# A cross-attention kernel: queries as seven products of halves, and the softmax's division applied to the product with the values

## The chip, the cores and the metric

The kernel runs on one core of a Trainium2 chip. The metric is the device time in microseconds (us) of one execution; lower is better. Times below are medians of several executions, or come from one execution that the hardware profiler recorded.

## The reference

There are 16 samples of 1024 query rows and 64 context rows, 512 features, 16 heads of 32. In short:

```python
xq  = (1 + scale_q(t)) * layernorm(x_q)  + shift_q(t)     # per sample: a scale and shift per feature
xkv = (1 + scale_kv(t)) * layernorm(x_kv) + shift_kv(t)
q   = xq @ Wq + bq                       # 1024 x 512 per sample
k,v = split(xkv @ Wkv + bkv)             # 64 x 512 each
attn = softmax(q k^T / sqrt(32))         # per head, over 64 keys
out  = x_q + (attn @ v) @ Wp + bp
```

Everything is float32.

## The kernel before

Work is cut into 32 blocks of 512 query rows, two for each sample. A block i passes through these stages, named by the functions that issue them:

- `load_x` brings x to SBUF; `q_stats`, `q_scale` and `hidden` normalise its rows (DVE statistics, small ACT and POOL steps, ACT normalising).
- `turn` transposes 32x32 squares on DVE into `ht`, and `move` puts them in their places with 16 DMAs between SBUF tiles, issued on SyncE's queue (SP). The result `xt` has features on partitions; its pool holds two buffers.
- `queries(i, o)` for o = 0 to 3 multiplies `xt` with weights that carry the sample's scale (`query_weights`, ACT, once for each sample): four matmuls on 512 columns for each o. ACT evicts each with its bias into `qt`.
- `scores(i, z)` for two halves z of the keys: 32x32-tiled matmuls into PSUM; DVE takes maxima per query and head, ACT copies the scores to SBUF. `maxima` spreads the maxima over the keys' partitions with one DVE transpose, `subtract` takes them off (POOL, two instructions of 128x2048), `weights` is the exponential (ACT, one for each z).
- `sums` adds up over keys (DVE, one for each z), `inverse` forms the reciprocals and spreads them (DVE transpose into `vb`), `divide` multiplies both halves of the weights by them (POOL, two instructions of 128x2048).
- `mix` multiplies with the values into PSUM (`po`).
- The projection with Wp is done as seven products of halves already (Strassen's scheme in Winograd's order): `mixed_halves` copies out of PSUM (ACT), `row_sums` and `last_row_sum` form sums of the mixed rows (DVE, one on POOL), `product(i, 1..7)` are the seven products, each 8 matmul instructions on 256 columns, in PSUM banks 2 and 3 seeded with the bias by `biased`, and `added(i, n)` adds each partial result to the residual `r` (DVE) and starts the output DMA.
- `context_features`, `keys`, `value_products` and `value_tiles` treat two samples' context once every four blocks.

A float32 matmul appears as two instructions in the profile. The whole kernel is one straight program whose order is written out by hand (`manual_schedule`): every engine and SP's queue execute their instructions in the order in which the Python code issues them, and wait on semaphores for the rest. The steady part is `for i in range(3, NB - 2)`, line 898. A "period" below is one turn of that loop: it does the scores of block i, the queries of block i+1, the mix and most of the projection of block i-1, the rest of the projection of i-2, the turning of i+2 and the load of i+3.

Instructions on one SP queue are all the loads, all the output stores and the 16 DMAs of each `move`.

Lines that the prediction uses: 487 query matmuls (`pq`), 504 their eviction (`qt`), 515 score matmuls (`ps`), 526 maxima, 533 score copies, 547 the spreads (`mb`, `vb`), 560 subtract, 566 exponential, 571 sums, 591 divide, 611 mix (`po`), 638 plain projection, 682 `residual_rest`, 702 and 703 `mixed_halves`, 710 to 714 `row_sums`, 719 `last_row_sum`, 740 the products (`pp`), 754 `added`, 756 the stores, 452 the DMAs of `move`, 132 and 139 the loads of x and of the residual, 169 small bias loads (`b_v_sb`), 347 and 375 the key and value products, 388 the values' eviction.

Of the kernel before, what the change touches and what calls it, by code (L numbers as in the profile page):

```python
# [15 lines left out]
P = 128  # L16
# [4 lines left out]
def cross_attention_block(  # L21
# [41 lines left out]

    nc = tc.nc
# [20 lines left out]
    big = ctx.enter_context(tc.tile_pool(name="big", bufs=4))  # L85
# [58 lines left out]
    def load_scale_shift(name, w):  # L144
        for j in range(2):
            t = big.tile([P, NC, H], F32, tag="big", name=f"wss_{name}_{j}")
            nc.sync.dma_start(t, w[:, j * H : (j + 1) * H].rearrange("(c p) o -> p c o", p=P))
            w_ss[name, j] = t
# [5 lines left out]
    at = 0  # L154
# [99 lines left out]
    def rstd_of(mv, n, tag, apart):  # L254
# [6 lines left out]
        rstd = small.tile([P, 2, n], F32, tag=f"rstd{tag}", name=f"rstd{tag}")  # L261
        work = small.tile([P, 4, n], F32, tag=f"work{tag}", name=f"work{tag}")
# [18 lines left out]
        return rstd  # L281

    q_mv, kv_mv, q_rstd, kv_rstd = {}, {}, {}, {}

    def q_stats(i, ts=range(NT)):
        if ts[0] == 0:
            q_mv[i] = small.tile([P, NT, 2], F32, tag="mvq", name=f"mvq_{i}")
        for t in ts:
            row_stats(q_mv[i][:, t, :], x_tiles[i][:, t, :])

    def q_scale(i):
        q_rstd[i] = rstd_of(q_mv.pop(i), NT, "q", i > 1)
# [5 lines left out]
    def kv_scale(b):  # L298
        kv_rstd[b] = rstd_of(kv_mv.pop(b), 1, "k", b > 0)
# [18 lines left out]
    def context_hidden(b):  # L318
        hk = kvpool.tile([P, H], F32, tag="hk", name=f"hk_{b}")
        normalise(hk, ctx_tiles.pop(b), kv_rstd.pop(b), 0)  # L320
        hk_tiles[b] = hk

    def context_features(b):
        hk = hk_tiles.pop(b)
        pt = bank(f"pkt_{b}")
        for c in range(NC):
            nc.tensor.transpose(pt[:, c * P : (c + 1) * P], hk[:, c * P : (c + 1) * P], ident)
        xk = kvpool.tile([P, NC, P], F32, tag="xk", name=f"xk_{b}")
# [11 lines left out]
        xk_tiles[b] = xk  # L340

    def keys(b):
        xk = xk_tiles[b]
        pk = bank(f"pk_{b}")
        for o in range(NC):
            for c in range(NC):
                nc.tensor.matmul(  # L347
                    pk[:, o * P : (o + 1) * P],
                    lhsT=w_kv_sb[:, c, o * P : (o + 1) * P],
                    rhs=xk[:, c, :],  # L350
                    start=(c == 0),
                    stop=(c == NC - 1),
                )
        kt = kvpool.tile([P, NC, P], F32, tag="kt", name=f"kt_{b}", bufs=2)
# [11 lines left out]
    def value_products(b):  # L366

        xk = xk_tiles.pop(b)
        pv = bank(f"pv_{b}").rearrange("p (j z f) -> p j z f", j=2, z=2)
# [107 lines left out]
    def queries(i, o, spare=False, later=False):  # L477

        xt, b = xt_tiles[i], i // BPB
        if o == 0:  # L480
            qt_tiles[i] = qpool.tile([P, NC, TB], F32, tag="qt", name=f"qt_{i}")
        if spare:
            pq = ps_s.tile([P, 2, TB], F32, tag="s", name=f"pq_{i}_{o}")[:, 0, :]
        else:
            pq = bank(f"pq_{i}_{o}")
        for c in range(NC):
            nc.tensor.matmul(  # L487
                pq.rearrange("p (g n) -> p g n", g=4),
                lhsT=wq_tiles[b][:, c, o * P : (o + 1) * P],
# [8 lines left out]
    def queried(i, o):  # L498
# [5 lines left out]
        nc.scalar.activation(dst, pq, AF.Identity, bias=bqs[:, o, b : b + 1])  # L504
# [3 lines left out]
    def scores(i, z):  # L508
# [15 lines left out]
        s_sb = big.tile([P, HPC, TB], F32, tag="big", name=f"s_{i}_{z}")  # L524
        for e in range(2):
# [6 lines left out]
            )  # L532
            nc.scalar.copy(s_sb[:, 2 * e : 2 * e + 2, :], pss[e])  # L533
        s_tiles[i, z] = s_sb
# [53 lines left out]
    def divide(i, eng=nc.gpsimd):  # L588
        vb = vb_tiles.pop(i)
        for z in range(2):  # L590
            eng.tensor_tensor(s_tiles[i, z], s_tiles[i, z], vb, ALU.mult)  # L591

# [64 lines left out]
    HO, HT, HC = H // 2, TB // 2, NC // 2  # L657
# [5 lines left out]
    def weight_sums():  # L663
        t1, t2, t3, t4 = (WT[:, j] for j in range(4))
        nc.gpsimd.tensor_tensor(t1, half_weights(0, 1), half_weights(0, 0), ALU.subtract)
        nc.gpsimd.tensor_tensor(t2, half_weights(1, 1), t1, ALU.subtract)
        nc.gpsimd.tensor_tensor(t3, half_weights(1, 1), half_weights(0, 1), ALU.subtract)
        nc.gpsimd.tensor_tensor(t4, half_weights(1, 0), t2, ALU.subtract)
        nc.gpsimd.tensor_tensor(b_diff, b_first, b_second, ALU.subtract)


# [4 lines left out]

    def twice(b):
        return b.unsqueeze(1).to_broadcast([P, 2, HO])

    def residual_rest(i):  # L680
        r = r_tiles[i][:, 2:, :HO]
        nc.gpsimd.tensor_tensor(r, r, twice(b_diff), ALU.add)

    acc = {}

    def biased(i):

        for k, n, b in ((2, 1, b_second), (3, 2, b_diff)):
            acc[k] = bank(f"pp_{i}_{n}", k)
            nc.scalar.copy(acc[k].rearrange("p (t h) -> p t h", t=2), twice(b))  # L690

# [6 lines left out]
    def mixed_halves(i):  # L698

        ot_tiles[i] = opool.tile([P, NC, TB], F32, tag="ot", name=f"ot_{i}")  # L700
        first, second = po_tiles[i]
        nc.scalar.copy(ot_tiles[i][:, HC:, :], second)
        nc.scalar.copy(half_rows(i, 0, 0), first[:, :, :HT])

    def row_sums(i):

        first = po_tiles.pop(i)[0]
        s1_tiles[i] = opool.tile([P, HC, HT], F32, tag="s1", name=f"s1_{i}")
        s2_tiles[i] = opool.tile([P, HC, HT], F32, tag="s2", name=f"s2_{i}")
        nc.vector.tensor_tensor(s1_tiles[i], first[:, :, HT:], half_rows(i, 1, 1), ALU.add)  # L710
        nc.vector.tensor_tensor(
            half_rows(i, 1, 0), half_rows(i, 0, 0), first[:, :, HT:], ALU.subtract
        )
        nc.vector.tensor_tensor(s2_tiles[i], s1_tiles[i], first[:, :, :HT], ALU.subtract)

    def last_row_sum(i):

        a12 = half_rows(i, 0, 1)
        nc.gpsimd.tensor_tensor(a12, a12, s2_tiles[i], ALU.subtract)

    def product(i, n, first=False):
# [4 lines left out]
            3: (lambda: half_rows(i, 0, 1), half_weights(1, 1)),  # L726
            4: (lambda: half_rows(i, 1, 1), WT[:, 3]),
            5: (lambda: s1_tiles.pop(i), WT[:, 0]),
            6: (lambda: s2_tiles[i], WT[:, 1]),
# [4 lines left out]
        new = n == 7 or first and n < 3  # L734
        if new:
            acc[k] = bank(f"pp_{i}_{n}", k)
        for t in range(2):
            for c in range(HC):
# [5 lines left out]
                    start=new and t == 0 and c == 0,  # L744
# [4 lines left out]
    def added(i, n):  # L749

        m, o = {1: (0, 0), 2: (0, 0), 6: (1, 0), 7: (1, 1), 5: (1, 1), 4: (1, 0), 3: (0, 1)}[n]
# [75 lines left out]
    queries(1, 3)  # L827
    sums(0, 1)
# [63 lines left out]
    residual(2, (0, 1))  # L892
    context_features(2)
    query_weights(2)
# [3 lines left out]
    for i in range(3, NB - 2):  # L898
        nxt3 = i + 3 < NB
        kvb = i // 4 * 2 + 2  # L900
        kv = i % 4 if kvb < B else None
        if nxt3:
            load_x(i + 3)
        if kv == 0:
            load_context(kvb)
        if i > 3:
            added(i - 2, 5)
        scores(i, 0)
        if i > 3:
            product(i - 2, 4)  # L910
            added(i - 2, 4)
            product(i - 2, 3)
            added(i - 2, 3)
        else:
            project(i - 2, 3)
            ring[:] = [0, 1]
        scores(i, 1)
        maxima(i)
        subtract(i)
        queries(i + 1, 0)  # L920
        load_residual(i)
        if i > 3:
            biased(i - 1)
        hidden(i + 2, (0, 1))
        mix(i - 1)
        mixed_halves(i - 1)
        hidden(i + 2, (2, 3))
        if kv == 1:
            context_hidden(kvb)
        if nxt3:  # L930
            q_stats(i + 3)
        if kv == 0:
            kv_stats(kvb)
        row_sums(i - 1)
        turn(i + 2, range(NT))
        move(i + 2)
        if not nxt3:
            load_residual(NB - 1)
        queries(i + 1, 1)
        product(i - 1, 1, first=i == 3)  # L940
        product(i - 1, 2, first=i == 3)
        weights(i, 0)
        added(i - 1, 1)
        added(i - 1, 2)
        sums(i, 0)
        weights(i, 1)
        queries(i + 1, 2)
        last_row_sum(i - 1)
        if i == 3:
            residual(2, (2, 3))  # L950
        if i < NB - 3:
            residual_rest(i)
        else:
            residual(i)
        product(i - 1, 6)
        product(i - 1, 7)
        sums(i, 1)
        added(i - 1, 6)
        inverse(i)
        added(i - 1, 7)  # L960
        divide(i)
        if nxt3:
            q_scale(i + 3)
        if kv == 0:
            kv_scale(kvb)
        if kv == 2:
            context_features(kvb)
        if kv == 3:
            keys(kvb)
        queries(i + 1, 3)  # L970
        if (i + 2) % BPB == 0 and i + 2 < NB:
            query_weights((i + 2) // BPB)
        if kv == 3:
            value_products(kvb)
            value_tiles(kvb)
        product(i - 1, 5)
# [4 lines left out]
    residual(z)  # L981
    added(y - 2, 5)
    scores(y, 0)
    product(y - 2, 4)
    added(y - 2, 4)
    product(y - 2, 3)
    added(y - 2, 3)
    ring[:] = [0, 1, 2, 3]
    load_residual(y)
    scores(y, 1)  # L990
    maxima(y)
    subtract(y, nc.vector)
    queries(z, 0)
    mix(y - 1)
    mixed(y - 1)
# [76 lines left out]
```

## Time and profile before

| | us |
|---|---|
| median of 3 runs | 1091.9 (1091.55 to 1092.94) |
| the profiled execution's own time | 1093.58 |
| span of its instructions | 1091.8 |
| busy: PE, weight loads (PEld) | 1073.8, 613.2 |
| busy: DVE, POOL, ACT | 872.9, 673.4, 602.6 |
| DMA engines, share busy | 41.4% |

Engines: PE is TensorE, DVE VectorE, ACT ScalarE, POOL GpSimd, SP SyncE. A row of a group of instructions reads: line, engine, operation, written tile `<-` read tiles, shapes, count | busy us in total, mean ns of one | idle time of that engine just before them, and what ended it. The chain is followed back from the last instruction, at each step to what released it. SPq rows are DMA issues on SP's queue: their duration is the time for which the queue was taken up with the issue, and "to landing" is the time from issue until the data's semaphore. The page's PE busy time counts waiting inside the pipeline, so the chain's pieces are the better price of a PE step.

### The profile page before, as it was taken

Reading aid. Unit: us, or ns where it says so; the run is one execution under the profiler, and the core shown is the slowest. Engines: PE = TensorE matmul, PEld = TensorE weight load, DVE = VectorE, ACT = ScalarE, POOL = GpSimd, SP = SyncE. Lnnn points to the kernel's source line nnn. Section 1 sums busy time; section 2 is a strip of 40 time slices with the busy share of each in tenths; the row PEclk is TensorE's granted clock in tenths of the full one; section 3 lists DMA queues with packets and bytes.
Section 4 is the critical chain, followed back from the end, with each engine's and each line's share of the span. In section 5 each row is a group of like instructions: output and inputs, shape, how many; then the busy total and the mean of one; then the engine's idle time right before and its main releaser. Section 6 shows DMA issues by size and latency. Waiting matters only on the chain.

```text
span 1091.8 us, 20467 instructions
## 1 busy us (share of the span) xinstructions
PE 1073.8 (98%) x8290; PEld 613.2 (56%) x8290; DVE 872.9 (80%) x1105; ACT 602.6 (55%) x895; POOL 673.4 (62%) x356
## 2 busy tenths in 40 slices
PE   6999999999999999999999999999999999999998
PEld 4534365555755557555566556555665555755533
DVE  5689678888698886989868889688887888697893
ACT  3665545656367572666736575465655656356430
POOL 0247786766748765666737766566765666748830
PEclk9999999999999999999999999999999999999999
DMA  9733532444334443444444443353442444333402
GB/s 338 241 110 116 153 116 103 145 152 149 94 111 144 142 145 113 122 127 142 138 141 128 117 140 126 131 155 121 131 143 91 145 156 136 97 111 100 137 30 87
DMA packets 80525, 145.36 MB, mean 133 GB/s; under 512 B 10504, under 2 KB 10656, under 8 KB 80432
## 3 DMA queue, kind: packets, MB, share of 16 engines
q1 hardware_dynamic: 80432, 144.07, 41.4%
q8 instruction: 65, 1.06, 0.4%
q14 instruction: 28, 0.23, 0.1%
HBM read 77.97 MB, written 33.55 MB: 102 GB/s over the span
## 4 chain that ended last, share of the span: by engine, by line
PE 92%; DMA 3%; DVE 3%; POOL 1%; SPq 1%; issue 0%; ACT 0%; DVEq 0%; POOLq 0%
PE pq L487 38%; PE pp L740 31%; PE po L611 6%; PE ps L515 6%; PE pp L638 6%; PE pv L375 2%; PE pk L347 2%; DMA wss_kv<-in_L_xcond_Wss_kv_dram 1%; DMA b_p_sb<-in_L_xcond_bp_dram 1%; POOL s L591 1%; DVE l L571 1%; DMA x<-in_x_dram 1%; SPq L452 0%; DVE vb L547 0%; DVE s L560 0%; DVE m L526 0%
## 5 line engine op out<-in xcount | busy, mean ns | idle before, releaser
L487 PE MATMUL pq<-xt,wq 128*128 128x512 f32 x1024 | 467.4, 600 | 2.2 <-DMA xt<-ht 1.1
L591 POOL TENSOR_TENSOR s<-s,vb 128x2048 f32<-128x2048 f32 x62 | 280.0, 4538 | 189.6 <-DVE vb L547 183.8
L560 POOL TENSOR_TENSOR s<-s,mb 128x2048 f32<-128x2048 f32 x58 | 262.8, 4554 | 136.7 <-DVE mb L547 136.7
L487 PEld LDWEIGHTS pq<-xt,wq 128*128 128x128 f32 x1024 | 188.8, 190 | 245.6 <-issue 240.4
L533 ACT COPY s<-ps 128x1024 f32<-128x1024 f32 x128 | 129.6, 1012 | 192.0 <-DVE m L526 184.5
L754 DVE TENSOR_TENSOR r<-pp,r 128x512 f32<-128x512 f32 x189 | 126.5, 669 | 69.9 <-PE pp L740 67.1
L504 ACT ACTIVATE qt<-pq,bqs 128x512 f32<-128x512 f32 x128 | 87.6, 685 | 153.0 <-PE pq L487 149.3
L526 DVE TRANSPOSE_TENSOR_REDUCE m<-ps 128x32 f32<-128x1024 f32 x128 | 152.2, 1227 | 24.6 <-PE ps L515 24.6
L566 ACT ACTIVATE s<-s 128x2048 f32<-128x2048 f32 x64 | 122.1, 1908 | 69.0 <-POOL s L560 63.7
L571 DVE TRANSPOSE_TENSOR_REDUCE l<-s 128x64 f32<-128x2048 f32 x64 | 146.6, 2301 | 6.5 <-ACT s L566 6.5
L740 PE MATMUL pp<-w_p_sb,ot 128*128 128x256 f32 x648 | 148.7, 379 | 0.0
L740 PEld LDWEIGHTS pp<-w_p_sb,ot 128*128 128x128 f32 x648 | 123.1, 190 | 28.3 <-ACT x L302 6.5
L740 PE MATMUL pp<-WT,ot 128*128 128x256 f32 x432 | 104.9, 386 | 0.0
L740 PE MATMUL pp<-WT,s 128*128 128x256 f32 x432 | 102.8, 381 | 0.0
L740 PEld LDWEIGHTS pp<-WT,s 128*128 128x128 f32 x432 | 81.5, 190 | 32.2 <-issue 20.8
L302 ACT ACTIVATE x<-x,rstdq 128x512 f32<-128x512 f32 x128 | 97.2, 811 | 3.9 <-POOL rstdq L274 2.2
L740 PEld LDWEIGHTS pp<-WT,ot 128*128 128x128 f32 x432 | 79.8, 190 | 32.4 <-DVE r L754 16.8
L251 DVE BATCH_NORM_STATS2 bs<-x 128x6 f32<-128x512 f32 x128 | 84.4, 660 | 3.9 <-DMA x<-in_x_dram 3.9
L439 DVE STREAM_TRANSPOSE ht<-x 128x512 f32<-128x512 f32 x124 | 77.5, 680 | 5.8 <-DMA xt<-ht 3.3
L547 DVE STREAM_TRANSPOSE mb<-m 128x2048 f32<-128x2048 f32 x32 | 74.0, 2311 | 6.7 <-POOL s L591 3.7
L515 PE MATMUL ps<-qt,kt 32*32 32x512 f32 x2048 | 76.1, 600 | 1.4 <-DVE kt L355 0.8
L547 DVE STREAM_TRANSPOSE vb<-v 128x2048 f32<-128x2048 f32 x32 | 74.0, 2311 | 3.0
(111 smaller groups left out, 871.2 us busy)
## 6 DMA issues: line engine op xcount, KB each, us to landing
x<-in_x_dram SPq DMA_DIRECT2D x32, 1024.0 KB, 5.6
r<-in_x_dram SPq DMA_DIRECT2D x32, 1024.0 KB, 5.5
xt<-ht SPq DMA_DIRECT2D x496, 64.0 KB, 2.0
out_dram<-r SPq DMA_DIRECT2D x54, 512.0 KB, 2.8
out_dram<-r SPq DMA_DIRECT2D x20, 256.0 KB, 2.0
wss_q<-in_L_xcond_Wss_q_dram SPq DMA_DIRECT2D x2, 1024.0 KB, 8.9
ctx<-in_ctx_dram SPq DMA_DIRECT2D x8, 256.0 KB, 5.5
wss_kv<-in_L_xcond_Wss_kv_dram SPq DMA_DIRECT2D x2, 1024.0 KB
```

Source lines behind the costliest of these rows:

```text
L302: nc.scalar.activation(dst, src, AF.Identity, bias=rstd[:, 1, j : j + 1], scale=rstd[:, 0, j : j + 1])
L487: nc.tensor.matmul(pq.rearrange("p (g n) -> p g n", g=4), lhsT=wq_tiles[b][:, c, o * P : (o + 1) * P], rhs=xt[:, :, c, :], start=(c == 0), ...
L515: nc.tensor.matmul(pss[r // 2][32 * c : 32 * c + 32, r % 2, :], lhsT=kt[rows, c, z * HK : (z + 1) * HK], rhs=qt[rows, c, :], start=True, s ...
L526: nc.vector.tensor_reduce(m_tiles[i][:, z, 2 * e : 2 * e + 2, :], pss[e].rearrange("p r (j a) -> p r j a", a=32), AX.X, ALU.max, apply_tra ...
L533: nc.scalar.copy(s_sb[:, 2 * e : 2 * e + 2, :], pss[e])
L547: nc.vector.transpose(t, src.unsqueeze(2).to_broadcast([P, HPC * NJ, 32]))
L560: eng.tensor_tensor(s_tiles[i, z], s_tiles[i, z], mb_tiles[i], ALU.subtract)
L566: nc.scalar.activation(p, p, AF.Exp, scale=SCALE)
L571: nc.vector.tensor_reduce(l_tiles[i][:, z], s_tiles[i, z].rearrange("p r (j a) -> p r j a", a=32), AX.X, ALU.add, apply_transpose=True,)
L591: eng.tensor_tensor(s_tiles[i, z], s_tiles[i, z], vb, ALU.mult)
L740: nc.tensor.matmul(acc[k][:, t * HO : (t + 1) * HO], lhsT=rows[:, c, t * P : (t + 1) * P], rhs=cols[:, c, :], start=new and t == 0 and c == 0,
L754: nc.vector.tensor_add(r, acc[k].rearrange("p (t h) -> p t h", t=2), r)
```

## The change

It has three parts. First, the queries of blocks 5 to 30 are formed as seven products of halves, from the unscaled weight `w_q_sb` and its sums (`query_weight_sums`, formed once on POOL): ACT scales and shifts `xt` in place (`scale_features`), POOL forms four sums of its halves (`feature_sums`), PE makes seven products of 8 instructions on 256 columns each in PSUM banks 0 and 1, ACT seeds one bank from the other (`query_seed`) and evicts (`query_out`), DVE adds the remaining quarter results (`query_added`). Blocks 0 to 4 and 31 keep `queries`.

Second, the weights are no longer divided before the mix. `total` adds the two key halves on POOL, `row_total` sums over keys on DVE, `inverse_rows` takes reciprocals and moves them into the mix's layout with 16 DMAs of 32 partitions x 16 numbers, `spread_rows` widens them with one DVE transpose, and `divided` multiplies the mix's PSUM result by them on DVE while it evicts it. All four row sums of the projection move to POOL, and its order of products and seeds changes (all of the bias comes by the seeds).

Third, the stages are spread over more periods: in period i the scores of i, the query products of n = i+1, the scaling and sums of f = i+2, the turning of i+3, the statistics of i+4 and the load of i+5; of the projection, a = i-1 and b = i-2 share the seven products (1, 2, 7 of a; 6, 5, 4, 3 of b). Context work goes to spare PSUM buffers of the scores' pool.

```diff
-    big = ctx.enter_context(tc.tile_pool(name="big", bufs=4))
+    big = ctx.enter_context(tc.tile_pool(name="big", bufs=1))
...
+    def scale_features(i, cs=range(NC)):
+        xt, b = xt_tiles[i], i // BPB
+        for c in cs:
+            nc.scalar.activation(
+                xt[:, :, c, :], xt[:, :, c, :], AF.Identity,
...
+    def feature_sums(i):
...
+        t = sums_of["xt"]
+        tt = nc.gpsimd.tensor_tensor
+        b12 = feature_half(i, 0, 1)
+        tt(t[:, 0], feature_half(i, 1, 1), b12, ALU.subtract)
+        tt(b12, b12, feature_half(i, 0, 0), ALU.subtract)
+        tt(t[:, 1], feature_half(i, 1, 1), b12, ALU.subtract)
+        tt(t[:, 2], feature_half(i, 1, 0), t[:, 1], ALU.subtract)
...
+    def query_product(i, n):
+        w, t = sums_of["wq"], sums_of["xt"]
+        a, x = {
+            1: (query_half(0, 0), feature_half(i, 0, 0)),
+            2: (query_half(0, 1), feature_half(i, 1, 0)),
+            3: (w[:, 3], feature_half(i, 1, 1)),
+            4: (query_half(1, 1), t[:, 2]),
+            5: (w[:, 0], feature_half(i, 0, 1)),
+            6: (w[:, 1], t[:, 1]),
+            7: (w[:, 2], t[:, 0]),
+        }[n]
+        k = 0 if n in (1, 6, 5, 3) else 1
...
+    def query_seed(i):
+        qa[1] = bank(f"pq_{i}_2", 1)
+        nc.scalar.copy(qa[1], qa[0])
...
+    def total(i):
+        t = big.tile([P, HPC, TB], F32, tag=f"big{(i + 1) % 2 * 2}", name=f"sum_{i}")
+        nc.gpsimd.tensor_tensor(t, s_tiles[i, 0], s_tiles[i, 1], ALU.add)
+        sum_tiles[i] = t
...
+    def inverse_rows(i):
+        lt = lt_tiles.pop(i)
+        nc.vector.reciprocal(lt, lt)
+        v = small.tile([P, NC, NJ], F32, tag="vr", name=f"vr_{i}")
+        for c in range(NC):
+            for r in range(HPC):
+                nc.sync.dma_start(v[32 * r : 32 * r + 32, c], lt[32 * c : 32 * c + 32, r])
+        vt_rows[i] = v
+
+    def spread_rows(i):
+        v = vt_rows.pop(i).rearrange("p c j -> p (c j)")
+        t = qpool.tile([P, NC, TB], F32, tag="vb", name=f"vb_{i}", bufs=1)
+        nc.vector.transpose(
+            t.rearrange("p c q -> p (c q)"), v.unsqueeze(2).to_broadcast([P, NC * NJ, 32])
+        )
+        vb_tiles[i] = t
+
+    def divided(i):
+        vb = vb_tiles.pop(i)
+        ot_tiles[i] = opool.tile([P, NC, TB], F32, tag="ot", name=f"ot_{i}")
+        for e in range(2):
+            cs = slice(2 * e, 2 * e + 2)
+            nc.vector.tensor_tensor(ot_tiles[i][:, cs, :], po_tiles[i][e], vb[:, cs, :], ALU.mult)
...
-    def biased(i):
+    def biased(i, k):
+        acc[k] = bank(f"pp_{i}_{k}", k)
+        b = b_first if k == 2 else b_diff
...
+    def row_sums(i, n):
+        tt = nc.gpsimd.tensor_tensor
+        if n == 0:
+            s1_tiles[i] = opool.tile([P, HC, HT], F32, tag="s1", name=f"s1_{i}")
+            tt(s1_tiles[i], half_rows(i, 1, 0), half_rows(i, 0, 0), ALU.subtract)
+            tt(half_rows(i, 1, 0), half_rows(i, 1, 1), half_rows(i, 1, 0), ALU.subtract)
+        else:
+            s2_tiles[i] = opool.tile([P, HC, HT], F32, tag="s2", name=f"s2_{i}")
+            tt(s2_tiles[i], half_rows(i, 1, 1), s1_tiles[i], ALU.subtract)
+            tt(half_rows(i, 0, 1), half_rows(i, 0, 1), s2_tiles[i], ALU.subtract)
```

The steady loop's new body (the old one is printed above; its lines are all removed):

```python
    for i in range(4, NB - 2):
        a, b, n, f = i - 1, i - 2, i + 1, i + 2
        ...
        scores(i, 0, crossed=True)
        product(b, 6)
        added(b, 6)
        inverse_rows(a)
        query_product(n, 1)
        query_seed(n)
        added(b, 7)
        scores(i, 1)
        product(b, 5)
        added(b, 5)
        maxima(i)
        subtract(i)
        product(b, 4)
        hidden(i + 3, (0, 1, 2))
        query_product(n, 2)
        query_out(n, 2)
        product(b, 3)
        spread_rows(a)
        hidden(i + 3, (3,))
        added(b, 4)
        added(b, 3)
        biased(a, 2)
        load_residual(i)
        mix(a)
        divided(a)
        row_sums(a, 0)
        query_product(n, 6)
        weights(i, 0)
        query_out(n, 6)
        ...
        scale_features(f, (0, 1))
        product(a, 1)
        turn(i + 3, (0,))
        added(a, 1)
        product(a, 2)
        turn(i + 3, (1,))
        added(a, 2)
        weights(i, 1)
        total(i)
        query_product(n, 7)
        query_out(n, 7)
        biased(a, 3)
        scale_features(f, (2, 3))
        row_sums(a, 1)
        ...                       # context: products of keys or values, by i % 4
        turn(i + 3, (2, 3))
        load_x(i + 5)
        q_stats(i + 4, (0, 1))
        query_product(n, 5)
        query_added(n, 5)
        q_stats(i + 4, (2,))
        ...
        query_product(n, 4)
        query_added(n, 4)
        q_stats(i + 4, (3,))
        query_product(n, 3)
        query_out(n, 3)
        feature_sums(f)
        product(a, 7)
        row_total(i)
        move(i + 3)
        q_scale(i + 4)
        ...
```

Period 3, which belonged to the loop, is written out ahead of it with plain queries. In the last two periods `inverse_rows`, `spread_rows` and `divided` take the place of the copies for block 29; blocks 30 and 31 keep the division of the weights.

## The prediction

> **What bounds the kernel now.** I read the page's busy times and slices first, then its chain.
>
> ```profile
> PE 1073.8 (98%) x8290; PEld 613.2 (56%) x8290; DVE 872.9 (80%) x1105; ACT 602.6 (55%) x895; POOL 673.4 (62%) x356
> PE   6999999999999999999999999999999999999998
> ...
> PE 92%; DMA 3%; DVE 3%; POOL 1%; SPq 1%; issue 0%; ACT 0%; DVEq 0%; POOLq 0%
> PE pq L487 38%; PE pp L740 31%; PE po L611 6%; PE ps L515 6%; PE pp L638 6%; PE pv L375 2%; PE pk L347 2%; DMA wss_kv<-in_L_xcond_Wss_kv_dram 1%; DMA b_p_sb<-in_L_xcond_bp_dram 1%; POOL s L591 1%; DVE l L571 1%; DMA x<-in_x_dram 1%; SPq L452 0%; DVE vb L547 0%; DVE s L560 0%; DVE m L526 0%
> ```
>
> TensorE (PE) is 98% busy, in every slice but the first and last, at full granted clock, and it carries 92% of the chain that ended last; SyncE's queue (SPq), whose 16-DMA batches matter below, carries 1%. Next I cut four successive periods of the loop out of the middle (each from one `load_residual` issue to the next) and asked for busy time by engine. Columns: length of the period, then busy us (instructions) of PE, weight loads, DVE, ACT, POOL, clock, DMA share, GB/s.
>
> ```profile
> 399.96:438.24 38.28, 38.28 (x378) 24.67 (x376) 28.05 (x37) 16.75 (x24) 21.32 (x10) 1.00 0.37 118
> 438.24:469.05 30.81, 30.81 (x217) 17.75 (x216) 27.17 (x36) 20.09 (x33) 21.59 (x12) 1.00 0.44 138
> 469.05:499.89 30.84, 30.84 (x217) 17.75 (x216) 26.56 (x34) 17.32 (x25) 21.75 (x13) 1.00 0.43 137
> 499.89:531.16 31.27, 31.27 (x221) 18.14 (x220) 26.54 (x34) 21.62 (x36) 21.33 (x10) 1.00 0.43 135
> ```
>
> PE fills every period. A plain period is 30.81 us; the first one, 38.28, holds the key and value products of a batch pair. DVE has 27.1 of 32.8 us, POOL 21.5, ACT 18.9. So the price of PE work is the price of the kernel, until another engine's chain becomes longer than a period. The chain of waits, in time order, prices the PE units (start, us, what):
>
> ```profile
> 439.26 2.28 PE po L611 x62
> ...
> 455.51 3.43 PE pq L487 x8
> 458.94 1.73 PE pp L740 x8
> 460.67 1.07 PE ps L515 x32
> ```
>
> A query step of 8 instructions on 512 columns takes 3.43, a product of 8 instructions on 256 columns 1.73, a scores half 1.07, the mix 2.28. Check: 4x3.43 + 7x1.73 + 2x1.07 + 2.28 = 30.25, so 0.56 goes to hand-overs.
>
> **The part that is easy to price: seven products.** The queries of a block now take 4x3.43 = 13.72; as seven products 7x1.73 = 12.11. That removes 1.6 us of PE from each block done that way: n = i+1 for i = 4 to 29, 26 blocks, 42 us. Half the columns cost half the time here: 1.73 is half of 3.43 within 0.02. [...] A PE-bound period would be 14x1.73 + 2.14 + 2.28 + 0.56 = 29.2.
>
> The other engines must cover the additions. DVE loses one of two `sums` (2.30), three row sums (2.03), one `both` (0.27); it gains `query_added`, four 128x256 (0.42 each by L388, 1.7), and `divided`, two 128x1024 from PSUM. The latter lies between L754's 0.67 for half the size and L560's 2.33 for twice the size in SBUF; I take 1.22, as L526 reads the same size from PSUM in 1.23. DVE: about 26.6 a period. POOL loses `divide` (9.1), `residual_rest` and `last_row_sum` (2.6), and gains `total` (4.5 by L591), four `row_sums` and four `feature_sums` (1.29 each by L719): 21.5 - 11.7 + 14.8 = 24.6. ACT loses `mixed_halves` (1.58) and `query_weights` (1.4 a period), gains `scale_features` (3.2), a seed copy (0.59) and about 0.5 of smaller evictions: 20. None of them fills 29.2, so each count is at nothing on the path; if a period were PE-bound, DVE's slack would be 2.6.
>
> **The part that decides: sixteen more DMAs on SP.** `inverse_rows(a)` turns the 128x64 reciprocals with 16 DMAs of 32 partitions x 64 bytes on SP's queue. SP's own timeline shows what such a batch takes (start, us, line, operation):
>
> ```profile
> 469.05 0.38 SPq L139 DMA_DIRECT2D r<-in_x_dram  x1
> 479.07 10.01 SPq L452 DMA_DIRECT2D xt<-ht  x16
> ...
> 509.89 10.02 SPq L452 DMA_DIRECT2D xt<-ht  x16
> ```
>
> The 16 DMAs of `move` hold SP for 10.01 us here; in the other periods shown 10.02 to 11.04, mean of five 10.5. Its line and its landings:
>
> ```profile
> L452 SPq DMA_DIRECT2D xt<-ht x496: 507/588/1624, 30.9 to 1013.7; - x166
> ...
> DMA to landing us min/median/max: 1.9/2.0/7.4
> ```
>
> A single one is 0.59, and with the step to the next some 0.63 passes. The wait for landing after the last issue is about 1.85: at 39.99 a batch's last six are issued until 44.44, and the DVE instruction that waits for them starts at 46.29.
>
> Now the order. SP is one queue. `move(i+3)` stands at the end of period i and writes the `xt` buffer (two of them) that block n = i+1 is still using: it must wait for `query_product(n,3)`, the last but one PE unit of the period. In the kernel before, `move` reused a buffer whose readers were long done and only waited for the transposes. Behind it in the queue stands the next period's `inverse_rows(a)`. Its reciprocal is ready early (some 4.8 us into the period), so it waits for SP, not for DVE. On DVE `spread_rows(a)` waits for all 16 landings, and behind it stand `added(b,4)`, `added(b,3)` and `divided(a)`; PE's `product(a,1)` needs the first half of `divided(a)`. Durations of DVE steps:
>
> ```profile
> L754 DVE TENSOR_TENSOR r<-pp,r 128x512 f32<-128x512 f32 x189 | 126.5, 669 | 69.9 <-PE pp L740 67.1
> ...
> L547 DVE STREAM_TRANSPOSE vb<-v 128x2048 f32<-128x2048 f32 x32 | 74.0, 2311 | 3.0
> ```
>
> From the end of `query_product(n,3)` to the start of `product(a,1)`: semaphore hop 0.2, `move` 10.5, `inverse_rows` 10.5, landing 1.85, spread 2.31, two adds 1.34, first half divided 1.22, hops 0.3. Sum 28.2. In the same stretch PE has eight products (13.84), two scores halves (2.14), mix (2.28), hand-overs 0.4: 18.7. So PE stands 9.5 us before `product(a,1)`, in every period, and the loop closes on itself: `query_product(n,3)` comes a fixed six products after `product(a,1)`, so the next `move` is as late again. Period 29.2 + 9.5 = 38.7 against 30.81: 7.9 more. Key and value products add the same to both kernels (they lie between `product(a,2)` and `query_product(n,5)`, on this loop, as they lie on PE's path before). Nothing else is later still: from the first half of `divided(a)` to the period's end DVE has 12.9 us of work (turns, adds, statistics, `row_total`) beside PE's 12.1, but the one step that PE needs from it there, `query_added(n,5)`, ends about 0.6 before its due time, and the 0.8 by which the next maxima start late is not on this loop; ACT, which waits in `biased(a,2)` behind `added(b,3)` with `weights(i,0)` behind it, and POOL's `total` and `row_sums` then fall 2 us inside their due times. SP itself has 21 + about 2 of issue in 38.7.
>
> The unknown is the issue time of a DMA of 32 x 64 bytes between two SBUF tiles. Bounds: the short loads at the start, 4 to 8 rows (0.28 and 0.29, step 0.33, 16 make 5.3); `move`'s own (step 0.63 plus a gap in each batch, 10.5); the slowest batch at the start 13.5. A gain from this term is excluded: before, no such DMA exists. I take 10.5: same count of partitions, same tile to tile form, on the same queue; only the bytes differ, and the 1 MB load `r`, 0.38, shows that bytes do not set issue time. The row has 0.59 of issue against 2.0 to landing, 16 times in series, and the sum goes by it. [...]
>
> Head and tail: the periods 0 to 3 keep plain queries; the last two periods have the same PE work, with one stall of a few us at `divided(y-1)` beside DVE's own subtraction. I put them at 0, bounds -5 and +10.
>
> Sum, against the profiled execution (1093.6; its span is 1091.8): 26 periods x 7.9 = 205, so 1299. The median of the runs, 1091.9, lies 1.7 below, so 1297.
>
> **Rivals.**
> 1. *PE stays the bound.* The batches are hidden and 26 x 1.6 = 42 is gained: 1050. For: DVE, POOL and ACT all fit. It needs the chain of 28.2 to be 18.7, that is, `inverse_rows` in 1.0 us or 0.06 a DMA; equality with the kernel before comes at a stall of 1.6, 2.6 us or 0.16 a DMA. No issue in the trace is under 0.28. Chance 0.09.
> 2. *A cheaper queue.* 64-byte rows issue at 0.33 (16 in 5.3: 1297 - 26x5.2 = 1162) or at 0.47, as `b_v_sb`'s loads of the same 32 partitions (7.5: 1219); or `move` is not held by `query_product(n,3)`, so only the second batch is on the path: reciprocal at 4.8, +10.5 +1.85 +2.31 +1.34 +1.22 +0.2 = 22.2 against 16.7, stall 5.5, 1193. Against: the rows above. Chance 0.17.
> 3. *DVE closes a second loop.* It works 26.6 and waits some 9 at the spread, 35.6 of 38.7; if `divided` costs 2.3 a half or landings come later, 1 to 2 us are added a period: 1323 to 1350. Chance 0.08.
> 4. *No change*: stall and saving cancel, 1092. Chance 0.01.
>
> Forecast 0.65. Range 1160 to 1345: from the lower end of rival 2 to most of rival 3, leaving out rival 1, no change and the rest above. Faster by over 0.2% (about what a measurement of this kernel can tell from no change) 0.09, within 0.01, slower 0.90.
>
> **What would show it.** In the profile of the changed kernel: PE busy near 80%, idle gaps of 9 to 10 us before the products of `ot` in each period, released by DVE `ot`; DVE idle before the spread `vb`, released by a DMA of `vr`, 8 to 10 us each; SP with two batches of 16 back to back, the first starting when a query product ends; SPq with over 40% of the chain. Right in part: a shorter second batch. Wrong: batches that don't touch, a spread that doesn't wait, or PE above 95% busy. Then rival 1 holds.

## The result, and the profile after

| | us |
|---|---|
| the changed kernel, median of 4 runs | 1352.8 (1348.2 to 1357.2) |
| the kernel before, on the same chip | 1092.1 (1091.6 to 1092.9) |
| ratio, 95% interval | 1.239 (1.233 to 1.244) |
| forecast | 1297 (1160 to 1345) |

The profiled execution took 1357.2 with a span of 1355.4. The change costs 261 us where 205 were forecast. The page's busy times, slices and chain of the changed kernel:

```profile
PE 1104.6 (81%) x8914; PEld 776.1 (57%) x8914; DVE 856.3 (63%) x1134; ACT 616.0 (45%) x951; POOL 752.7 (56%) x470
PE   7999977887778877798777977779777897778898
...
PEclk9999988988889888998889988899888988889899
...
SPq 35%; PE 29%; DVE 12%; issue 8%; DMA 7%; POOL 4%; ACT 4%; DVEq 0%; POOLq 0%; ACTq 0%
SPq L786 18%; SPq L506 17%; PE pq L623 10%; PE pp L930 10%; DVE vb L792 5%; PE pp L849 4%; DMA vr<-lt 3%; ACT s L733 2%; PE pq L540 2%; DVE r L944 2%; PE pk L393 2%; DVE ot L802 2%; POOL s L758 1%; DVE m L683 1%; DMA wss_kv<-in_L_xcond_Wss_kv_dram 1%
```

PE is busy 81% of the span, and no engine has taken its place: DVE has 63%, POOL 56%. The chain now runs through SP's queue (35%; it was 1%). Its two lines are the two batches of DMAs, L506 `move` and L786 `inverse_rows`. The clock row (PEclk: the TensorE clock that was granted, in tenths of full speed; 9 is 90% or more) now shows 8 in many slices. It had none in the kernel before; that row was not thought of in the forecast and turns out to matter. The same row of before:

```profile
PEclk9999999999999999999999999999999999999999
```

SP's own timeline (start, us, line, operation, count) through two periods:

```profile
547.74 11.14 SPq L506 DMA_DIRECT2D xt<-ht  x16
558.98 10.04 SPq L786 DMA_DIRECT2D vr<-lt  x16
573.25 0.99 SPq L946 DMA_DIRECT2D out_dram<-r  x2
...
588.67 10.99 SPq L506 DMA_DIRECT2D xt<-ht  x16
599.76 10.24 SPq L786 DMA_DIRECT2D vr<-lt  x16
```

The batches touch. Each pair takes 21.2 us of a period of 40.9, and the rest of the period the queue is almost empty. What `move` (L506 here, L452 before) waited for on the queue, first in the kernel before, then in the changed one (us in total, times, longest):

```profile
SPq L452 <- DVE ht L439: 286.6, 29, 20.1
```

```profile
SPq L506 <- PE pq L623: 172.6, 25, 14.6
```

Before, it waited for the transposes; now it waits for a query product, in 25 periods, as the forecast had it. What the second batch consists of, by its source line (min/median/max ns, then the times to landing):

```profile
L786 SPq DMA_DIRECT2D vr<-lt x432: 507/588/1702, 175.0 to 1286.7; - x144
...
DMA to landing us min/median/max: 1.6/1.7/3.7
```

The median issue is 588 ns, the same as for `move`'s DMAs of 32 times as many bytes. DVE then spreads, adds and divides, and PE starts on the first half (timeline of DVE, then of PE; in brackets the idle time before and its releaser):

```profile
570.34 2.31 DVE L792 STREAM_TRANSPOSE vb<-vr 128x2048 f32<-128x2048 f32 x1 [9.60 <-DMA vr<-lt]
572.58 1.25 DVE L944 TENSOR_TENSOR r<-pp,r 128x512 f32<-128x512 f32 x2
573.75 2.34 DVE L802 TENSOR_TENSOR ot<-po,vb 128x1024 f32<-128x1024 f32 x2
```

```profile
575.10 6.15 PE L930 MATMUL pp<-w_p_sb,ot 128*128 128x256 f32 x16 [8.60 <-DVE ot L802]
581.09 1.89 PE L623 MATMUL pq<-xt_sums,wq_sums 128*128 128x256 f32 x8
```

The waits over the whole span (us in total, times, longest) say how regular that is:

```profile
DVE vb L792 <- DMA vr<-lt: 254.1, 27, 11.0
...
PE pp L930 <- DVE ot L802: 227.1, 26, 10.0
```

26 waits of PE, 8.7 each, one in every period. In the timeline of PE above there is a second loss: the two products after the gap (16 instructions) take 6.15, while two products took 3.62 in this row of PE's timeline of before:

```profile
406.77 3.62 PE L740 MATMUL pp<-w_p_sb,ot 128*128 128x256 f32 x16
```

The next product takes 1.89 again. The windows around that moment show why (us, busy by engine, PE's granted clock, DMA share, GB/s; first the gap, then the first 4.5 us of work, then the rest up to the next `product(a,7)`):

```profile
566.50:575.10 8.60, 0.00 (x0) 0.03 (x1) 4.76 (x5) 1.24 (x2) 3.45 (x2) 0.69 0.13 41
575.10:579.60 4.50, 4.50 (x11) 3.60 (x12) 2.24 (x4) 4.50 (x7) 2.48 (x2) 0.50 0.57 190
579.60:588.44 8.84, 8.84 (x44) 7.75 (x42) 7.24 (x17) 4.08 (x6) 7.36 (x4) 0.97 0.68 222
```

The clock falls while PE is idle (its mean over this gap is 0.69) and is still 0.50 for the first 4.5 us of work: 11 instructions are done there, 0.41 each, against 44 in the 8.84 that follow, 0.20 each. In the trace's clock records the half-clock spells of the steady part last 10.24 us, and one comes in each period; 3.2 to 6.2 us of each, some 5 in the mean, lie over PE's work.

Cut at the first maxima of block 4 and of block 30, the span goes: head 168.6 before and 169.0 after, steady part 848.7 and 1104.3, tail 74.4 and 82.1. So the steady part lost 255.6, which is 9.8 a period where 7.9 were forecast, and the tail 7.7.

### The profile page after: what moved, and what is told of

Its sections match the earlier page's. It is cut to its first block, busy times and chain, and to the rows that moved or that the text cites. A ratio compares the mean times of both kernels' runs of the same rounds, so it can differ in the third digit from the quotient of the medians.

```text
span 1355.4 us, 22762 instructions
## 1 busy us (share of the span) xinstructions
PE 1104.6 (81%) x8914; PEld 776.1 (57%) x8914; DVE 856.3 (63%) x1134; ACT 616.0 (45%) x951; POOL 752.7 (56%) x470
## 4 chain that ended last, share of the span: by engine, by line
SPq 35%; PE 29%; DVE 12%; issue 8%; DMA 7%; POOL 4%; ACT 4%; DVEq 0%; POOLq 0%; ACTq 0%
SPq L786 18%; SPq L506 17%; PE pq L623 10%; PE pp L930 10%; DVE vb L792 5%; PE pp L849 4%; DMA vr<-lt 3%; ACT s L733 2%; PE pq L540 2%; DVE r L944 2%; PE pk L393 2%; DVE ot L802 2%; POOL s L758 1%; DVE m L683 1%; DMA wss_kv<-in_L_xcond_Wss_kv_dram 1%
## 5 line engine op out<-in xcount | busy, mean ns | idle before, releaser
L930 PE MATMUL pp<-w_p_sb,ot 128*128 128x256 f32 x648 | 216.8, 504 | 227.1 <-DVE ot L802 227.1
L930 PEld LDWEIGHTS pp<-w_p_sb,ot 128*128 128x128 f32 x648 | 168.1, 264 | 272.1 <-ACT pp L893 236.8
L792 DVE STREAM_TRANSPOSE vb<-vr 128x2048 f32<-128x2048 f32 x27 | 62.4, 2311 | 254.1 <-DMA vr<-lt 254.1
L683 DVE TRANSPOSE_TENSOR_REDUCE m<-ps 128x32 f32<-128x1024 f32 x128 | 154.1, 1235 | 29.2 <-PE ps L671 29.2
L653 ACT ACTIVATE qt<-pq,bias_t 128x256 f32<-128x256 f32 x208 | 86.1, 464 | 182.7 <-PE pq L623 182.7
L766 POOL TENSOR_TENSOR sum<-s,s 128x2048 f32<-128x2048 f32 x27 | 122.6, 4541 | 72.7 <-ACT s L733 72.7
L733 ACT ACTIVATE s<-s 128x2048 f32<-128x2048 f32 x64 | 121.9, 1904 | 14.7 <-DVE s L727 10.4
L905 POOL TENSOR_TENSOR s<-ot 128x512 f32<-128x512 f32 x27 | 34.5, 1277 | 137.0 <-DVE ot L802 137.0
L623 PE MATMUL pq<-xt_sums,wq_sums 128*128 128x256 f32 x416 | 101.0, 386 | 0.0
L623 PE MATMUL pq<-xt,wq_sums 128*128 128x256 f32 x416 | 98.9, 381 | 0.0
L623 PE MATMUL pq<-xt,w_q_sb 128*128 128x256 f32 x416 | 98.3, 379 | 0.7 <-PE pp L930 0.7
L623 PEld LDWEIGHTS pq<-xt_sums,wq_sums 128*128 128x128 f32 x416 | 76.9, 190 | 31.2 <-issue 21.8
```

What stands on the lines that cost most here:

```text
L623: nc.tensor.matmul(qa[k][:, m * HT : (m + 1) * HT].rearrange("p (g n) -> p g n", g=2), lhsT=a[:, c, m * P : (m + 1) * P], rhs=x[:, :, c, : ...
L683: nc.vector.tensor_reduce(m_tiles[i][:, z, 2 * e : 2 * e + 2, :], pss[e].rearrange("p r (j a) -> p r j a", a=32), AX.X, ALU.max, apply_tra ...
L733: nc.scalar.activation(p, p, AF.Exp, scale=SCALE)
L766: nc.gpsimd.tensor_tensor(t, s_tiles[i, 0], s_tiles[i, 1], ALU.add)
L792: nc.vector.transpose(t.rearrange("p c q -> p (c q)"), v.unsqueeze(2).to_broadcast([P, NC * NJ, 32]))
L930: nc.tensor.matmul(acc[k][:, t * HO : (t + 1) * HO], lhsT=rows[:, c, t * P : (t + 1) * P], rhs=cols[:, c, :], start=n == 2 and t == 0 and ...
```

## The experiments

**What the second batch costs: leave it out, or half of it.** The theory: SP's two batches in series close the loop, so that without the second the PE-bound version remains (1050), and half of it gives back half. The rival: DVE's own work or something else in the new order closes the loop, and the time stays over 1095 without the batch and near 1350 with half of it.

First all 16 DMAs out:

```diff
-        v = small.tile([P, NC, NJ], F32, tag="vr", name=f"vr_{i}")
-        for c in range(NC):
-            for r in range(HPC):
-                nc.sync.dma_start(v[32 * r : 32 * r + 32, c], lt[32 * c : 32 * c + 32, r])
-        vt_rows[i] = v
+        vt_rows[i] = lt
```

> The 16 DMAs of inverse_rows are left out: spread_rows reads the reciprocals where they are, so the division uses the wrong rows; every engine's work is as in the changed kernel. Theory: no stall, TensorE sets the period again at 29.2: about 1050. Rival (the added DVE and POOL work, not SP's queue, sets the time): the period stays over 31 and the time over 1095.

Measured: 1058.1, ratio 0.968 (0.967 to 0.970). The page:

```profile
PE 1033.2 (98%) x8914; PEld 732.0 (69%) x8914; DVE 855.7 (81%) x1134; ACT 617.6 (58%) x951; POOL 753.2 (71%) x470
```

PE is at 98%, with all the other work of the change still there. The whole loss, and the hidden gain, hang on these 16 DMAs. Then 8 of the 16:

```diff
+        nc.vector.memset(v, 0.0)
...
-        for c in range(NC):
+        for c in range(2):
```

> Eight of the 16 DMAs of inverse_rows are issued, the other half of their tile is set to zero, so two quarters of the result are left out. Theory: 8 x 0.66 = 5.3 us less on the chain in each of 26 periods, 138; the idle time falls to 3.3 us, and if the clock then stays up, another 60: 1155 to 1215. Rival (one DMA's latency counts, not the number of issues): about 1350.

Measured: 1203.5, ratio 1.102 (1.100 to 1.104). SP's timeline and the waits:

```profile
567.87 10.72 SPq L506 DMA_DIRECT2D xt<-ht  x16
578.68 4.98 SPq L787 DMA_DIRECT2D vr<-lt  x8
```

```profile
PE pp L931 <- DVE ot L803: 89.6, 25, 5.3
```

Half of the DMAs take half of the queue's time (4.97 in the mean, 5.3 less), PE's gap falls from 8.8 to 3.6 (5.2 less), and 149 us come back, 5.7 a period. The gap accounts for 5.2 of that; from the start of `product(a,1)` to the next `move` 14.6 us pass instead of 15.1, and the clock of the run is 0.952 instead of 0.900. So the clock did not stay up: it still fell around pauses of 3.6 in the mean.

**Whether the clock after the gap is the missing part.** The theory: the six products after the gap were priced at full clock, and the half clock is what lies between 1297 and 1353; with PE kept at work in the gap the time falls to about 1290 although nothing else is shortened. The rival: something else delays these products, then filling the gap makes no difference. The first filler did the mix four times over, 96 more small matmuls a period, 192 instructions:

```diff
-        for z in range(2):
-            p = s_tiles.pop((i, z))
+        ps = [s_tiles.pop((i, z)) for z in range(2)]
+        for z in list(range(2)) * times:
+            p = ps[z]
...
-        mix(a)
+        mix(a, times=4)
```

> The mix of each period of the steady loop is computed four times instead of once (the same result each time), so that TensorE works 6.8 us of the 8.6 us in which it stood idle before the first product of block a; nothing else changes. Theory (SP's two batches in series set the idle time; after the idle time TensorE runs some 4.6 us of work at half clock, which costs 2.3 us a period): more work, less time: the clock stays at 1.0 and the time falls by 26 x 2.3 = 60 to about 1293. Rival (the 2.2 us a period above the forecast come from DVE closing a second loop): the clock is beside the point, the time stays at 1350 or rises.

Measured: 1369.4, ratio 1.254 (1.251 to 1.257): a miss, 17 us slower than without the filler. It did not do what it was for. PE still stood 3.7 us before `product(a,1)` in the mean (2.2 to 5.1), and the clock still fell in some periods and not in others. Two rows of PE's timeline show the same 16 instructions after the same gap of 2.44:

```profile
576.21 3.69 PE L931 MATMUL pp<-w_p_sb,ot 128*128 128x256 f32 x16 [2.44 <-DVE ot L802]
...
659.37 5.38 PE L931 MATMUL pp<-w_p_sb,ot 128*128 128x256 f32 x16 [2.44 <-DVE ot L802]
```

The first ran at a granted clock of 1.00 (576.21 to 587.31), the second window, 659.37 to 674.00, at 0.88. So the link from clock to duration held; what failed was the filler. It also made the second batch on SP longer, 11.3 against 10.3 in the mean, and the wait for landing 1.8 against 1.4. Why the batch of DMAs on SP took longer beside these additional matmuls on PE was not settled.

The second filler used few, wide matmuls, ten of 512 columns into the mix's own PSUM banks ahead of the mix, which then overwrites them:

```diff
+            for k in range(filler):
+                nc.tensor.matmul(
+                    po[k % NC].rearrange("p (g n) -> p g n", g=4),
+                    lhsT=w_q_sb[:, k % NC, :P],
+                    rhs=xt_tiles[i + 2][:, :, k % NC, :],
+                    start=True,
+                    stop=True,
+                )
...
-        mix(a)
+        mix(a, filler=10)
```

> As in the first filling run, TensorE is given work that no result needs, now 10 matmuls of 128x128 by 512 columns (20 instructions, about 8.6 us) ahead of the mix of block a, so that its idle time before the first product goes from 8.8 us to about 0, with few instructions added. Theory (half clock after idle time costs the 2.8 us by which the work from product(a,1) to the next move exceeds its 10.4): the granted clock stays at 1.0, the sum from the end of one move batch to the start of the next falls by 2.8 a period: 1353 - 26 x 2.8 = 1280, with more work done. Rival (the 2.8 come from DVE): clock up, time unchanged at 1345 to 1360.

Measured: 1289.0, ratio 1.179 (1.177 to 1.182). The page, a window of 120 us in the middle (its clock is 1.00), and PE's waits for `ot`:

```profile
PE 1258.8 (98%) x9434; PEld 828.8 (64%) x9434; DVE 857.3 (67%) x1134; ACT 615.8 (48%) x951; POOL 752.8 (58%) x470
```

```profile
600.00:720.00 120.00, 119.68 (x923) 83.49 (x922) 79.73 (x108) 57.52 (x91) 70.90 (x46) 1.00 0.35 105
```

```profile
PE pp L938 <- DVE ot L802: 4.3, 10, 0.7
```

More work for PE (the filler's group is 227 us busy), and 64 us less time. The chain from `move` to `product(a,1)` takes 27.4, where it took 27.5; from `product(a,1)` to the next `move` it is 12.6 instead of 15.1, and 26 times 2.55 is 66. This is the missing part. The run also shows a trap: PE is 98% busy, but with work that no result needs. The filler fills the gap almost exactly: in 10 periods PE still waits for `ot`, in the other 16 the filler ends last, by 0.17 us a period in the mean.

**Whether the order on SP matters.** `inverse_rows(i)` moved from behind the next scores to behind `row_total(i)`, ahead of `move(i+3)`:

```diff
         row_total(i)
+        inverse_rows(i)
         if i + 3 < NB:
             move(i + 3)
...
-        inverse_rows(a)
```

> Only the order on SP's queue is changed: inverse_rows(i) is issued at the end of period i, right behind row_total(i) and ahead of move(i+3), instead of behind it. Theory (move's batch stands in front of the reciprocals' batch on one queue): 10.85 us leave the old loop; a new one appears, reciprocal batch 10.3, move 10.85, landing 1.9, scaling of the features 1.6, exponential 1.9, total 4.55, row_total 2.3, reciprocal 0.53, hops 0.6 = 34.5 a period against 42.5 on average now: 26 x 8 = 208 less, 1125 to 1180. Rival (the latency or the shape of these DMAs costs, not the queue's order): about 1350.

Measured: 1165.7, ratio 1.067 (1.064 to 1.069). SP's timeline and the two longest waits for a DMA:

```profile
556.73 10.50 SPq L786 DMA_DIRECT2D vr<-lt  x16
567.34 11.23 SPq L506 DMA_DIRECT2D xt<-ht  x16
```

```profile
DVE ht L493 <- DMA xt<-ht: 146.4, 27, 6.3
...
ACT xt L563 <- DMA xt<-ht: 117.1, 27, 5.2
```

Same DMAs, same queue time, 187 us less. The spread no longer waits for `move`; instead `move` waits for the reciprocals, and the steps behind it are late. The period came out near the 34.5 that were expected (35.1, or 912.9 over 26), but the new loop was not only the expected one: besides ACT's scaling, DVE's next `turn` waits, since `ht` has one buffer and `move` must have read it.

**The version without the queue.** The same 16 copies as POOL instructions:

```diff
-                nc.sync.dma_start(v[32 * r : 32 * r + 32, c], lt[32 * c : 32 * c + 32, r])
+                nc.gpsimd.tensor_copy(v[32 * r : 32 * r + 32, c], lt[32 * c : 32 * c + 32, r])
```

> The 16 DMAs of inverse_rows become 16 copies of 32 partitions x 16 numbers on POOL, which is idle until the maxima are spread; by POOL's small steps (0.20 each, 0.30 apart) they take about 4.8 us from the reciprocal on and end 1 to 2 us ahead of the spread. Nothing is left out. Theory: no stall, about 1050, below both kernels. Rival (DVE or POOL is the bound): over 1095.

Measured: 1061.2 (1060.2 to 1063.3), ratio 0.972 (0.971 to 0.974). It beats both kernels. The page, its chain, and the copies and the spread in the timelines of POOL and DVE:

```profile
PE 1032.3 (98%) x8914; PEld 731.2 (69%) x8914; DVE 857.1 (81%) x1134; ACT 617.6 (58%) x951; POOL 838.2 (79%) x902
...
PE 84%; POOL 5%; DMA 4%; DVE 4%; SPq 2%; issue 1%; ACT 1%; POOLq 0%; DVEq 0%
```

```profile
482.74 3.66 POOL L786 COPY vr<-lt 32x16 f32<-32x16 f32 x16
```

```profile
486.43 2.31 DVE L792 STREAM_TRANSPOSE vb<-vr 128x2048 f32<-128x2048 f32 x1 [0.22 <-POOL vr L786]
```

16 copies take 3.66 on an engine that had room for them, and of the 21 us of queue `move` alone is left. PE is the bound again, at the forecast PE-bound period: 29.2 in the plain ones.

One more variant moved `residual(z)` behind `inverse_rows(y-1)` in the tail, so that the copies go ahead of it on POOL.

> The kernel with POOL's copies, and one step of the tail moved: residual(z), four POOL instructions of 1.24 us, stands behind the last block's copies of reciprocals instead of ahead of them. Nothing is left out. Theory (in the last-but-one period these 5 us of POOL stand on the chain ahead of the copies, the spread and a query step): 4 to 5 us less, 1056. Rival (the tail is held by something else): 1061.

Measured: 1059.5 (1058.6 to 1059.9), ratio 0.970 (0.968 to 0.972). The tail is 82.4 instead of 84.5, the direction as expected, but the intervals of the two ratios overlap.

**What the seven products are worth.** With the POOL copies in place, the queries as four plain steps again. The first attempt put the steps where the products had been:

```diff
-        query_product(n, 1)
-        query_seed(n)
...
-        query_product(n, 2)
-        query_out(n, 2)
+        queries(n, 0)
...
```

> The kernel with POOL's copies, but with the queries of blocks 5 to 30 as four products of 512 columns again (no sums of features on POOL, no seed, no adds on DVE); all else as there. Nothing is left out. Theory (the seven products are worth 1.6 us of TensorE in each of 26 blocks and nothing else gains): 1061 + 42 = 1103, with a period of 30.8. Rival (the gain comes from the new division or the spreading of the stages): near 1061.

Measured: 1120.8, ratio 1.026 (1.024 to 1.027), 18 above what was expected. With `query_product(n,1)` gone only one product lies between the two scores halves, and PE comes to the second half before DVE and ACT have emptied the bank. The chain of waits (start, us, what):

```profile
571.87 1.26 DVE m L683
573.13 0.02 issue
573.15 1.02 ACT s L692
```

The second attempt moved `product(b,5)` between the halves as cover.

> As in the run with plain queries and POOL's copies, but product(b,5) stands ahead of scores(i,1), so that two products instead of one cover the reading of the first scores half (there TensorE waited some 0.65 a period for DVE's maxima and ACT's copies). Nothing is left out. Theory (seven products are worth 1.6 us a block, and the rest of that run's 60 us was this wait): 1061 + 26 x 1.6 = 1103, period 30.8. Rival (the new division needs the sums' slack of the seven products): still about 1120.

Measured: 1142.7, ratio 1.046 (1.045 to 1.048), worse still: product 5 goes into the PSUM bank that `added(b,6)` has yet to read, and this waits on DVE behind the maxima. The wait, 36 us in 26 periods, is

```profile
PE pp L930 <- DVE r L944: 35.9, 26, 6.0
```

The third put the first plain step itself between the halves (`queries(n, 0, later=True)` there, its eviction `queried(n, 0)` after).

> Plain queries with POOL's copies once more, now with the first query step (3.43 of TensorE) between the two scores halves, where the seven products have one of 1.73, and its eviction behind the second half; no product is moved. Nothing is left out. Theory (the seven products are worth 1.6 us in each of 26 blocks, and the two runs before paid for waits of their own): 1061 + 42 = 1103, period 30.8. Rival (plain queries cost more here for another reason): over 1115.

Measured: 1102.2 (1101.3 to 1104.5), ratio 1.010 (1.008 to 1.012). The chain through its middle is PE alone, as it is in the kernel before. Against the POOL version, 1061.2, the seven products are worth 41 us, 1.6 a period. What is left against the kernel before, 10 us, is not in the steady part (846.4 here, 848.7 before) but in the tail, 84.6 against 74.4.

## Why the prediction came out as it did, point by point

**The bound before, and the price of a product: held.** The saving of 1.6 a block was measured as 41 us in all against 42. The PE-bound period of 29.2 is what the POOL version runs at; over the steady part it has 804.8 where the kernel before had 848.7.

**The covers: held.** DVE 26.7, POOL 24.6 and ACT 19.8 in the plain period from 547.74 to 588.67, against 26.6, 24.6 and 20. Half a `divided` took 1.21 (taken: 1.22), a `query_added` 0.42. These rows came from the nearest shapes of the trace before.

**The second batch: held.** The estimate of 10.5 for 16 DMAs that the trace before did not contain came out at 10.28, and the row chosen for it (same partitions, tile to tile, same queue) was the right one; the short loads at 0.33 were not. Issuing takes 0.59 against 1.7 to landing for one DMA here, and 10.3 against 1.4 of further waiting for 16 in a row: the kernel without these DMAs ran at 1058, with them at 1353.

**The chain that closes the loop: held, 0.7 too long.** Mean of 22 periods: hop 0.3, `move` 10.9, `inverse_rows` 10.3, landing 1.4, spread to the first product 4.8, together 27.5 from the start of `move`, against 28.2. PE's gap was 8.8 against 9.5. Leaving the batch out, halving it and swapping the order each moved the time as the chain says. No run freed `move` from the query product (a third buffer for `xt`, say); that link rests on SP's waits above.

**"`query_product(n,3)` comes a fixed six products after `product(a,1)`": the price of this step failed.** At 1.73 each, as the sum has them, six products are 10.4; that is the price of PE's pieces in a kernel that does not pause in its steady part. After the pauses of 8.8 us here PE did not run at that price. The stretch to the next `move` took 15.1 in the mean, of which 1.9 are key, value and context products, so 13.2 instead of 10.4. With the gap filled it took 12.6, less 1.9: 10.7. So 2.55 of the 2.8 are the clock, shown by the run with the wide filler. The other 0.3 is mostly the hop from the query product to `move`, which the forecast counted in its 28.2: at 588.44 PE starts on the next product, at 588.67 `move` begins. An estimate from the trace's clock records gives the same: of the 10.24 us of a spell 5.1 lie over work in the mean of the 22 periods, and at a granted clock of 0.50, where an instruction took 0.41 instead of 0.20, half of this, 2.55, is lost. Which pauses slow the work after them was not shown: in the run with the small filler the same pause of 2.44 was followed by a slow stretch in one period (two products in 5.38) and by none in another (3.69).

**The tail at 0: 7.7 too low, within the bounds of -5 and +10.** "The same PE work" was wrong by two products: of block 28, products 6, 5, 4 and 3 now come after the steady part, where only 4 and 3 did before. That is 3.5 us. The rest was not taken apart.

**The sum.** 26 times (2.8 less 0.7) is 55, and 8 more come from the tail and the head (7.7 and 0.4): 1297 becomes 1360. The steady part as a whole gives 50 (9.83 less 7.9, times 26) instead of 55, as the 22 periods are not all of the 26. For the profiled execution, where 1299 was forecast, that is 1357, and it took 1357.2, as it must, since the three parts were cut from it; the median of the four runs, 1352.8, is 4.4 lower. The chain, 0.7 too long, made up for a part of what the six products were priced too low; the run with the wide filler, at full clock, took 1289, 8 below the forecast.

**The rivals.** The measured time lies just beyond the 1323 to 1350 of the third rival, DVE as a second loop, but its mechanism is excluded: DVE is 63% busy with the work that was forecast, half a `divided` is not dearer, landings came sooner, and with the same DVE work the wide filler took 64 us off. The first rival, PE as the bound, had its point of decision right: it needs the second batch off the queue, and with that it is what runs. The second rival did not occur: the batch was no cheaper (10.28), and `move` is held by a query product.

**What would show it.** PE near 80%: 81%. Gaps of 9 to 10 released by DVE `ot`: 8.7. Idle before the spread of 8 to 10: 9.4. Batches back to back: yes. SPq over 40% of the chain: 35% of the whole, since head and tail are in it too.

## What to carry to other kernels

Count the DMAs on a queue, not their bytes (2 KB and 64 KB both took 0.59 us to issue here): multiply the count by the issue time of one, add what stands ahead in the same queue and what that waits for, and see whether the step that needs the data has that long. If the data are a few small squares between partitions, an engine with room to spare may do it with plain copies: 3.7 us instead of 10.3 here, and out of the queue. Where a forecast puts a pause like the 8.8 us here on PE, price the work after it at half clock for some 5 us (5.1 at 0.50 here), or it comes out too cheap; and a PE that is 98% busy may still be filling a gap.

## What the hardware showed that had not been expected

A pause of 8.8 us on PE cost 2.55 us more after its end, by a granted clock of 0.50, and pauses of 2.2 to 5.1 in the run with the small filler cost something in some periods and nothing in others (after two pauses of 2.44 two products took 5.38 and 3.69). Each of the 26 half-clock spells of the changed kernel began 2.9 to 4.4 us after PE had fallen idle; after a pause of 2.44 in the run with the small filler one began 1.2 us after PE had gone back to work. With 96 additional small matmuls a period, on PE alone, SP's batch of 16 DMAs took 11.3 us in the mean instead of 10.3; with ten wide ones it took 10.3. A copy of 32 x 16 numbers from one group of 32 partitions to another took 0.19 us on POOL (the median; 16 took 3.66), a third of what its DMA took to issue.
